# Three score banks allocated once and rotated by hand, with one head's exp and the other head's scores issued in two parts

## The chip, the cores and the metric

The kernel runs on one core of a Trainium2 chip. The metric is the device time of one execution in microseconds (us), and a version's time is the median of several runs. The engines are named as in the profile: PE (TensorE matmuls), PEld (its weight loads), DVE (VectorE), ACT (ScalarE), POOL (GpSimd) and SP (SyncE, which issues DMAs).

## The reference

Eight sequences of 1024 tokens with 256 features go through a causal attention of 16 heads of 16 features, and then through a mixture of 8 experts of which each token takes 2. All is float32. Cut to what matters:

```python
x = x + layernorm(attention(layernorm(x)))
    # q, k, v = x Wq^T, x Wk^T, x Wv^T, split into 16 heads of 16
    # score = q k^T / 4, causal; attn = softmax(score); out = (attn v) Wo^T
x = x + layernorm(moe(layernorm(x)))
    # scores = softmax(x Wr^T + br); the 2 best of 8 experts
    # gate, up = x Wgu[e] + bgu[e]; gate = min(gate, 7); up = clip(up, -7, 7)
    # down = ((up + 1) * gate * sigmoid(1.702 gate)) Wd[e] + bd[e], weighted by the scores
```

## The kernel before

The work has two parts. Attention comes first (to about 1395 us of the profile), with the routing of the tokens woven into it; then the experts' tiles follow.

In attention the unit of work `u` is one sequence and a group of four heads: 8 sequences by 4 groups are 32 units. The four heads of a group lie on four groups of 32 rows of PE, so that four matmuls with 32 rows each can run side by side. Each unit is gone through twice, one unit apart. The first pass (`maxima_tiles`, tiles `sa`, matmul L834) makes scores with queries on partitions, and DVE takes the row maxima (L844, L850, L859, L865); with them goes an edge copy on ACT (L869). The maxima become one more row of the queries `qP` by a DMA (L807). The second pass (`values_tiles`, tiles `sb`, matmul L929) makes the scores again, with keys on partitions and the maximum already subtracted; ACT takes the exp (L941) out of the score bank into the tile `pT` in the on-chip memory, POOL masks the diagonal blocks (L950), and PE multiplies by the values (L970, `weighted`), one or more steps later.

A unit has nine steps (`STEPS`): two EDGE steps, three TWO steps and four WHOLE steps. In an EDGE or a WHOLE step, each head has one score matmul of 512 columns in the second pass; in a TWO step it has two, of 384 and 128 or of 256 and 256 columns, that share one bank. Each step is done for two pairs of heads. One pass through the inner loop (L1328 to L1341) therefore issues a set of four heads: two of `sa` of unit `u` and the other two of `sb` of unit `u - 1`, in the order sa head 0, sa head 1, sb head 0, sb head 1. Then ACT's exps of the set are issued, and after them the reductions and the edge copy of `sa`. Between sets PE gets `av` matmuls and pieces of side jobs (projections L740, values L726, output projection L1031, transposes L574 and L1092, routing).

The order of PE, DVE, ACT and SP is the order of the source: the attention part is a list written out by the loop, in which side jobs are put in by estimated costs and due times (`pump`, `spend`). These estimates are not measured in the run, so the order is fixed when the kernel is built. POOL's order is held to the source by added dependencies (`in_order`).

The scores of `sb` and all the side jobs' PSUM tiles come from one pool, `ps_b` (L540), of three buffers of one PSUM bank (512 float32 for each of 128 partitions):

```python
ps_b = ctx.enter_context(tc.tile_pool(name="ps_b", bufs=3, space=PSUM))
...
banks = [
    ps_b.tile([P, QC], F32, tag="b", name=f"sb_{u}_{k}_{2 * pair + hh}")
    for hh in range(2)
]
...
for hh in range(2):
    nc.scalar.activation(pT[:, 2 * pair + hh, :], banks[hh], AF.Exp)
```

The pool hands out its three buffers in turn. A set takes two of them; so where no side job takes one in between, the second `sb` head of a set gets the bank that the first `sb` head of the set before had, and waits until its exp has read it. Where one side job took a bank in between, the two heads get the banks of the same heads of the set before. In the last unit the second pair of heads uses a bank pair of another pool (`ps_a`) and one exp of 1024 columns (L938). The experts' part goes on using `ps_b` for its second product (`dn`, L1497).

Of the kernel before, what the change touches and what calls it, by code (L numbers as in the profile page):

```python
# [11 lines left out]
F32 = mybir.dt.float32  # L12
# [5 lines left out]
P = 128  # L18
# [40 lines left out]
def attn_moe_kernel(  # L59
# [241 lines left out]
    def table(nr):  # L301
# [56 lines left out]
        yield piece(pe=0.6, dve=0.2, after=3 if first_ones else 5)  # L358
        ps = ps_b.tile([P, 3], F32, tag="b", name=f"segps_{nr}")
        if first_ones:  # L360
# [8 lines left out]
        yield piece(pe=0.3, dve=0.9, after=2)  # L369
        ps = ps_b.tile([P, 3], F32, tag="b", name=f"firstps_{nr}")  # L370
        nc.tensor.matmul(ps[:, 0:2], lhsT=before, rhs=seg[:, 0:2], start=True, stop=True)
# [43 lines left out]
        yield piece(pe=0.5, dve=0.6, after=2 if first_ones else 5)  # L415
        ps = ps_b.tile([P, 2, NTILES], F32, tag="b", name=f"tabps_{nr}")
        nc.tensor.matmul(
# [8 lines left out]
        if first_ones:  # L426

            yield piece(dve=0.9)
            some = tp.tile([P, 1], F32, tag="some", name=f"some_{nr}")
            nc.vector.tensor_scalar(  # L430
                some, ends[:, 0:1], -1.0, float(EARLY), ALU.mult, ALU.add
            )
            nc.vector.tensor_scalar(some, some, 0.0, seg[:, 0:1], ALU.max, ALU.min)
            each = tp.tile([P, E], F32, tag="each", name=f"each_{nr}")
            nc.vector.tensor_scalar(each, of_e, some, None, ALU.mult)
            yield piece(pe=0.3, dve=0.2, after=1)
            ps = ps_b.tile([P, E], F32, tag="b", name=f"takenps_{nr}")
            nc.tensor.matmul(ps, lhsT=ones, rhs=each, start=True, stop=True)
            nc.vector.tensor_copy(taken, ps)
# [99 lines left out]

    ps_b = ctx.enter_context(tc.tile_pool(name="ps_b", bufs=3, space=PSUM))  # L540

    with ExitStack() as attn:
# [28 lines left out]
        def turn_x(b, t, xn, kt):  # L571
            ps = ps_b.tile([P, NTB, P], F32, tag="b", name=f"xps_{b}_{t}_{kt}")
            for n in range(NTB):
                nc.tensor.transpose(ps[:, n, :], xn[:, n, ts(kt, P)], ident)  # L574
            nc.scalar.copy(xnTs[b][:, kt, ts(t, TB)], ps.rearrange("p n c -> p (n c)"))

        def weights(name, wr, kt):

            ps = ps_b.tile([P, KT, P], F32, tag="b", name=f"wps_{name}_{kt}")
            for ot in range(KT):  # L580
                nc.tensor.transpose(ps[:, ot, :], wr[:, ot, ts(kt, P)], ident)
            nc.scalar.activation(
                wT[name][:, kt, :], ps.rearrange("p t o -> p (t o)"), AF.Copy,
                scale=DH**-0.5 if name == "q" else 1.0,
            )
# [82 lines left out]
        def others(wr):  # L668
# [14 lines left out]
            yield piece(pe=0.3, dve=0.2)  # L683
            ps = ps_b.tile([P, KT, E], F32, tag="b", name="rps")
            for kt in range(KT):
                nc.tensor.transpose(ps[:, kt, :], rwr[:, ts(kt, P)], ident[:E, :E])
            nc.vector.tensor_copy(rw32[:, :, :E], ps)
            yield piece(pe=0.2, dve=0.4)
            ps = ps_b.tile([P, E * 2 * FT], F32, tag="b", name="gubps")
            nc.tensor.transpose(ps, gubr, ident[: E * 2 * FT, : E * 2 * FT])  # L690
# [27 lines left out]
        def values(b):  # L718

            xnT = xnTs[b]  # L720
            for n2 in range(NB // 2):
                yield piece(pe=1.75, act=0.6, after=0 if n2 else 1)
                ps = ps_b.tile([P, 2, D], F32, tag="b", name=f"vps_{b}_{n2}")
                for k in range(2):
                    for kt in range(KT):
                        nc.tensor.matmul(  # L726
                            ps[:, k, :], lhsT=xnT[:, kt, ts(2 * n2 + k, P)], rhs=wT["v"][:, kt, :],
                            start=(kt == 0), stop=(kt == KT - 1),
                        )
                nc.scalar.copy(  # L730
                    vps[b % 2][:, ts(n2, 2), : H * VS].rearrange(
                        "p n (h c) -> p n h c", c=VS
                    )[:, :, :, :DH],
                    ps.rearrange("p n (h d) -> p n h d", d=DH),
                )

        def project_chunk(b, g2, name, c):
            ps = ps_b.tile([P, QC], F32, tag="b", name=f"pj{name}_{b}_{g2}_{c}")
            for kt in range(KT):
# [159 lines left out]
        def values_tiles(u):  # L899
# [11 lines left out]
            def pair_of_heads(k, pair):  # L911
# [3 lines left out]
                if u == B * NG - 1 and pair:  # L915
                    both = ps_a.tile([P, 2, QC], F32, tag="a", name=f"sb_{u}_{k}_{pair}")
                    banks = [both[:, hh, :] for hh in range(2)]
                else:
                    banks = [
                        ps_b.tile([P, QC], F32, tag="b", name=f"sb_{u}_{k}_{2 * pair + hh}")  # L920
                        for hh in range(2)
                    ]

                def scores(hh, part):
                    if part == len(STEPS[k][2]):
                        return
                    c, j, off, at = list(parts(k))[part]
                    r = ds((2 * pair + hh) * HS, HS)
                    nc.tensor.matmul(  # L929
                        banks[hh][:, ds(at, QC - off)], lhsT=kP[r, ts(j, P)],  # L930
                        rhs=qP[r, ds(c * QC + off, QC - off)],
                        start=True, stop=True,
                    )

                def exps():
                    if u == B * NG - 1 and pair:

                        nc.scalar.activation(pT[:, ts(pair, 2), :], both, AF.Exp)  # L938
                        return
                    for hh in range(2):  # L940
                        nc.scalar.activation(pT[:, 2 * pair + hh, :], banks[hh], AF.Exp)  # L941

# [74 lines left out]
        def finish(b, c):  # L1017
# [8 lines left out]
            for n2 in range(NTB // 2):  # L1026
                yield piece(pe=1.75, act=0.6, after=0 if n2 else 2)
                ps = ps_b.tile([P, 2, D], F32, tag="b", name=f"yps_{b}_{c}_{n2}")
                for k in range(2):
# [44 lines left out]
        def route(t, x1, last):  # L1074
# [13 lines left out]
            for kt in range(KT):  # L1088
                yield piece(pe=0.5, act=0.6, after=0 if kt else 2)
                ps = ps_b.tile([P, NTB, P], F32, tag="b", name=f"x2ps_{t}_{kt}")  # L1090
                for n in range(NTB):
# [3 lines left out]
            yield piece(pe=0.6, act=0.3, after=1 + 2 * more)  # L1095
            ps = ps_b.tile([P, P], F32, tag="b", name=f"lpsT_{t}")
            for kt in range(KT):
# [7 lines left out]
            yield piece(pe=0.2, dve=0.2, after=1 + more)  # L1105
            lps = ps_b.tile([P, NTB, HS], F32, tag="b", name=f"lps_{t}")
            nc.tensor.transpose(lps.rearrange("p n r -> p (n r)"), lgT, ident)
# [42 lines left out]
            yield piece(pe=0.6, dve=0.2, after=1 + 4 * more)  # L1150
            cps = ps_b.tile([P, 2, NTB, E], F32, tag="b", name=f"cps_{t}")
            for k, m in enumerate((before, ones)):
# [335 lines left out]
    def lower_half(i, act, wd, bs, final=False):  # L1488
# [7 lines left out]
        else:  # L1496
            ps = ps_b.tile([P, TN, D], F32, tag="b", name=f"dn_{i}")  # L1497
            pss = [ps[:, n : n + 1, :] for n in range(TN)]
# [263 lines left out]
```

## Time and profile before

| what | value |
|---|---|
| median of 3 runs | 2196.28 us (2194.48 to 2196.68) |
| the profiled execution | 2198.81 us, span 2197.1 us |
| mean granted PE clock | 0.978 |
| instructions in the span | 44652 |
| exps of 512 columns (L941) | 1134, mean 596 ns, 616.6 us busy |
| matmul records of `sb` (L929) | 3072, 717.1 us busy |
| matmul records of `sa` (L834) | 3072, 658.7 us busy |
| ACT waiting for L929 before L941 | 361.2 us |
| PE's first waiting weight load of L929 for L941 | 20.3 us in 32 waits |

The span is the time from the first to the last instruction of the profiled execution; its own time is 1.7 us longer. A float32 matmul leaves two records, one for each pass over its columns. An instruction's length includes its way through the engine, so two that follow each other on one engine overlap in the records. A wait is listed only where the engine stood idle; PE is busy as long as any of its row groups works.

### The profile page before, as it was taken

Reading aid. Unit: us, or ns where it says so; the run is one execution under the profiler, and the core shown is the slowest. Engines: PE = TensorE matmul, PEld = TensorE weight load, DVE = VectorE, ACT = ScalarE, POOL = GpSimd, SP = SyncE. Lnnn points to the kernel's source line nnn. Section 1 sums busy time; section 2 is a strip of 40 time slices with the busy share of each in tenths; the row PEclk is TensorE's granted clock in tenths of the full one; section 3 lists DMA queues with packets and bytes.
Section 4 is the critical chain, followed back from the end, with each engine's and each line's share of the span. In section 5 each row is a group of like instructions: output and inputs, shape, how many; then the busy total and the mean of one; then the engine's idle time right before and its main releaser. Section 6 shows DMA issues by size and latency. Waiting matters only on the chain.

```text
span 2197.1 us, 44652 instructions
## 1 busy us (share of the span) xinstructions
PE 2085.6 (95%) x16205; PEld 1273.3 (58%) x16205; DVE 1713.9 (78%) x4090; ACT 1061.2 (48%) x2068; POOL 1058.0 (48%) x1217
## 2 busy tenths in 40 slices
PE   7999999999999999999999988899999999999995
PEld 4444444444444444444434433577788888888884
DVE  4786887887896886886887788567868888877776
ACT  3566665666666655665655654423123232222222
POOL 3421742572564455465454445455545444444443
PEclk9999999999999999999999998999999999999998
DMA  4101112111212112111112111645777767776784
GB/s 122 22 17 42 39 26 57 36 50 36 48 43 50 29 37 64 27 48 46 48 36 55 29 47 35 201 167 201 227 262 255 280 241 271 277 247 223 271 273 157
DMA packets 147096, 254.85 MB, mean 116 GB/s; under 512 B 21504, under 2 KB 106008, under 8 KB 144952
## 3 DMA queue, kind: packets, MB, share of 16 engines
q1 hardware_dynamic: 133128, 217.01, 32.1%
q0 software_dynamic: 12528, 34.36, 4.2%
q8 instruction: 129, 2.11, 0.4%
q14 instruction: 95, 0.78, 0.1%
q10 hardware_dynamic: 1216, 0.58, 0.1%
HBM read 171.13 MB, written 55.63 MB: 103 GB/s over the span
## 4 chain that ended last, share of the span: by engine, by line
PE 67%; DVE 20%; POOL 6%; issue 4%; ACT 1%; DMA 1%; another core or an unknown queue 0%; SPq 0%; DVEq 0%; ACTq 0%; POOLq 0%
PE sa L834 18%; PE gu L1461 13%; PE av L970 10%; PE dn L1501 7%; PE sb L929 6%; PE pjk L740 3%; PE yps L1031 3%; PE vps L726 3%; PE pjq L740 3%; DVE mx L850 2%; DVE sa L844 2%; DVE acc L1576 1%; POOL ytd L1514 1%; DVE gate L1470 1%; DVE act L1482 1%
## 5 line engine op out<-in xcount | busy, mean ns | idle before, releaser
L941 ACT ACTIVATE pT<-sb 128x512 f32<-128x512 f32 x1134 | 616.6, 596 | 399.8 <-PE sb L929 361.2
L929 PE MATMUL sb<-qP,kP 32*128 32x512 f32 (+3 forms) x3072 | 717.1, 530 | 11.3 <-ACT pT L941 6.5
L834 PE MATMUL sa<-kP,qP 32*128 32x512 f32 (+3 forms) x3072 | 658.7, 529 | 23.5 <-DVE mx L844 10.8
L1461 PE MATMUL gu<-xsT,wg 128*128 128x256 f32 (+1 forms) x2208 | 488.9, 374 | 5.8 <-DVE act L1482 3.7
L1461 PEld LDWEIGHTS gu<-xsT,wg 128*128 128x128 f32 x2208 | 409.3, 191 | 61.6 <-ACT sig L1472 4.1
L850 DVE TENSOR_REDUCE mx<-sa 128x2 f32<-128x1024 f32 x256 | 310.9, 1216 | 127.0 <-PE sb L929 100.6
L950 POOL TENSOR_SCALAR_AFFINE_SELECT pT<-pT 128x512 f32<-128x512 f32 x256 | 163.1, 652 | 474.7 <-ACT pT L941 462.1
L834 PEld LDWEIGHTS sa<-kP,qP 32*128 32x128 f32 x3072 | 228.8, 186 | 247.5 <-issue 104.7
L1472 ACT ACTIVATE sig<-gate 128x256 f32<-128x256 f32 (+1 forms) x276 | 112.8, 409 | 531.6 <-DVE gate L1470 485.6
L970 PE MATMUL av<-pT,vpad 128*32 128x256 f32 (+1 forms) x5120 | 350.1, 370 | 5.9 <-DVE avs L981 4.3
L929 PEld LDWEIGHTS sb<-qP,kP 32*128 32x128 f32 x3072 | 298.6, 187 | 54.8 <-ACT pT L941 20.3
L1477 POOL TENSOR_TENSOR sig<-sig,gate 128x256 f32<-128x256 f32 (+1 forms) x276 | 198.7, 722 | 256.3 <-ACT sig L1472 253.9
L970 PEld LDWEIGHTS av<-pT,vpad 128*32 128x32 f32 x5120 | 116.8, 109 | 296.5 <-issue 238.7
L1501 PE MATMUL dn<-wd,act 128*128 128x256 f32 x1064 | 263.0, 387 | 13.8 <-DVE act L1482 13.3
L1470 DVE TENSOR_SCALAR gate<-gu,bs 128x256 f32<-128x256 f32 (+1 forms) x276 | 128.9, 467 | 124.7 <-PE gu L1461 110.0
L1501 PEld LDWEIGHTS dn<-wd,act 128*128 128x128 f32 x1064 | 197.1, 193 | 48.1 <-DVE act L1482 24.2
L844 DVE CUSTOM_DVE_ANT_0 sa<-sa,cmask 128x512 f32<-128x512 f32 x256 | 177.7, 698 | 43.0 <-PE sb L929 20.8
L1514 POOL DMA_INDIRECT ytd<-ys,places x133 | 133.8, 1006 | 130.1 <-DVE ys L1509 93.8
L1194 POOL DMA_INDIRECT xsd<-xn,slots x128 | 127.9, 999 | 64.0 <-DVE xn L1190 34.0
L1482 DVE SCALAR_TENSOR_TENSOR act<-up,sig 128x256 f32<-128x256 f32 (+1 forms) x276 | 123.2, 446 | 27.1 <-POOL sig L1477 27.1
L869 ACT COPY edge<-sa 128x512 f32<-128x512 f32 x192 | 113.0, 589 | 35.8 <-DVE mx L859 16.5
L517 POOL TENSOR_TENSOR rstd<-ve,nhalf_seg 128x4 f32<-128x4 f32 x48 | 50.2, 1045 | 163.3 <-DVE ve L512 161.6
(243 smaller groups left out, 2416.8 us busy)
## 6 DMA issues: line engine op xcount, KB each, us to landing
wg<-_L_ffn_gate_up_proj_dram SPq DMA_DIRECT2D x69, 1024.0 KB
wd<-in_L_ffn_down_proj_dram SPq DMA_DIRECT2D x69, 512.0 KB
xs<-xsd SPq DMA_DIRECT2D x60, 258.0 KB
yy<-ytd SPq DMA_DIRECT2D x15, 1024.0 KB
bs<-biasd SPq DMA_DIRECT2D x69, 132.0 KB
x<-in_L_attn_x_dram SPq DMA_DIRECT2D x16, 512.0 KB
aT<-avn SPq DMA_DIRECT2D x256, 32.0 KB
x1d<-y SPq DMA_DIRECT2D x16, 512.0 KB
```

Of the source, the lines that this page charges most:

```text
L834: nc.tensor.matmul(ps[:, hh, ds(at, w)], lhsT=qP[r, ts(i, P)], rhs=kP[r, ds(c * QC, w)], start=True, stop=True,)
L844: nc.vector.tensor_tensor_reduce(out=ps[:, hh, :], in0=ps[:, hh, :], in1=cmask, scale=1.0, scalar=NEG, op0=ALU.add, op1=ALU.max, accum_out ...
L850: nc.vector.tensor_reduce(mx[:, heads, i, 2:3], ps, AX.X, ALU.max)
L929: nc.tensor.matmul(banks[hh][:, ds(at, QC - off)], lhsT=kP[r, ts(j, P)], rhs=qP[r, ds(c * QC + off, QC - off)], start=True, stop=True,)
L941: nc.scalar.activation(pT[:, 2 * pair + hh, :], banks[hh], AF.Exp)
L950: in_order(nc.gpsimd.affine_select(out=d, in_=d, compare_op=ALU.is_ge, fill=0.0, base=0, pattern=[[0, HG], [1, P]], channel_multiplier=-1,))
L970: nc.tensor.matmul(av[ds(hh * HS, HS), ds(off + a - at, z - a)], lhsT=vp[:, j, ds((g * HG + hh) * VS, HS)], rhs=pT[:, hh, a:z],  start=c n ...
L1461: nc.tensor.matmul(ps[:, half, :w], lhsT=wg[:, kt, ds(half * FF + f * P, P)], rhs=xT[:, kt, :], start=(kt == 0), stop=(kt == KT - 1),)
L1470: nc.vector.tensor_scalar(gt, ps[:, 0, :w], bs[:, f : f + 1], LIMIT, ALU.add, ALU.min)
L1477: in_order(nc.gpsimd.tensor_tensor(sg, sg, gt, ALU.mult))
L1501: nc.tensor.matmul(pss[n][:, 0, :], lhsT=act[:, f, ts(n, P)], rhs=wd[:, f, :], start=(f == 0), stop=(f == FT - 1),)
L1514: put = nc.gpsimd.indirect_dma_start(out=yt_dram[:, :], out_offset=bass.IndirectOffsetOnAxis(ap=places[:, i, n : n + 1], axis=0), in_=y[:, ...
```

## The change

The pool `ps_b` gets one buffer, and three tiles of a whole bank are taken from it once, at the start. A function `bank` hands out the first of them, cut to the shape asked for, and moves it to the end of the row. Every place that took a tile from `ps_b` calls it instead (side jobs, routing, `sb` and `dn`).

In `values_tiles` the exp of the first head of a pair is issued as two instructions of 256 columns each, in all steps. The scores of the second head of a pair are issued as two matmuls of 256 columns each where the step has one part (EDGE and WHOLE); in a TWO step they stay as they were. The exp of the second head stays one instruction of 512 columns.

```diff
-    ps_b = ctx.enter_context(tc.tile_pool(name="ps_b", bufs=3, space=PSUM))
+    ps_b = ctx.enter_context(tc.tile_pool(name="ps_b", bufs=1, space=PSUM))
+    banks = deque(ps_b.tile([P, 2 * D], F32, name=f"bank{i}") for i in range(3))
+
+    def bank(parts, *free):
+        at = banks[0]
+        banks.rotate(-1)
+        size = 1
+        for n in free:
+            size *= n
+        at = at[:parts, :size]
+        if len(free) == 2:
+            return at.rearrange("p (a b) -> p a b", b=free[1])
+        if len(free) == 3:
+            return at.rearrange("p (a b c) -> p a b c", b=free[1], c=free[2])
+        return at
...
-            ps = ps_b.tile([P, QC], F32, tag="b", name=f"pj{name}_{b}_{g2}_{c}")
+            ps = bank(P, QC)
...
-                    banks = [
-                        ps_b.tile([P, QC], F32, tag="b", name=f"sb_{u}_{k}_{2 * pair + hh}")
-                        for hh in range(2)
-                    ]
+                    into = [bank(P, QC) for hh in range(2)]
+                half = QC // 2
+
+                def pieces(hh, part):
+                    c, j, off, at = list(parts(k))[part]
+                    if hh and len(STEPS[k][2]) == 1:
+                        return [(c, j, off, at, half), (c, j, off + half, at + half, half)]
+                    return [(c, j, off, at, QC - off)]
 
                 def scores(hh, part):
                     if part == len(STEPS[k][2]):
                         return
-                    c, j, off, at = list(parts(k))[part]
                     r = ds((2 * pair + hh) * HS, HS)
-                    nc.tensor.matmul(
-                        banks[hh][:, ds(at, QC - off)], lhsT=kP[r, ts(j, P)],
-                        rhs=qP[r, ds(c * QC + off, QC - off)],
-                        start=True, stop=True,
-                    )
+                    for c, j, off, at, w in pieces(hh, part):
+                        nc.tensor.matmul(
+                            into[hh][:, ds(at, w)], lhsT=kP[r, ts(j, P)],
+                            rhs=qP[r, ds(c * QC + off, w)],
+                            start=True, stop=True,
+                        )
...
-                    for hh in range(2):
-                        nc.scalar.activation(pT[:, 2 * pair + hh, :], banks[hh], AF.Exp)
+                    for at in range(2):
+                        nc.scalar.activation(
+                            pT[:, 2 * pair, ts(at, half)], into[0][:, ts(at, half)], AF.Exp
+                        )
+                    nc.scalar.activation(pT[:, 2 * pair + 1, :], into[1], AF.Exp)
```

More of the change, by code (lines that the diff above doesn't have):

```diff
@@ L358, in table @@
         yield piece(pe=0.6, dve=0.2, after=3 if first_ones else 5)
-        ps = ps_b.tile([P, 3], F32, tag="b", name=f"segps_{nr}")
+        ps = bank(P, 3)
         if first_ones:
@@ L369, in table @@
         yield piece(pe=0.3, dve=0.9, after=2)
-        ps = ps_b.tile([P, 3], F32, tag="b", name=f"firstps_{nr}")
+        ps = bank(P, 3)
         nc.tensor.matmul(ps[:, 0:2], lhsT=before, rhs=seg[:, 0:2], start=True, stop=True)
@@ L415, in table @@
         yield piece(pe=0.5, dve=0.6, after=2 if first_ones else 5)
-        ps = ps_b.tile([P, 2, NTILES], F32, tag="b", name=f"tabps_{nr}")
+        ps = bank(P, 2, NTILES)
         nc.tensor.matmul(
@@ L436, in table @@
             yield piece(pe=0.3, dve=0.2, after=1)
-            ps = ps_b.tile([P, E], F32, tag="b", name=f"takenps_{nr}")
+            ps = bank(P, E)
             nc.tensor.matmul(ps, lhsT=ones, rhs=each, start=True, stop=True)
@@ L571, in turn_x @@
         def turn_x(b, t, xn, kt):
-            ps = ps_b.tile([P, NTB, P], F32, tag="b", name=f"xps_{b}_{t}_{kt}")
+            ps = bank(P, NTB, P)
             for n in range(NTB):
@@ L577, in weights @@
         def weights(name, wr, kt):
-            ps = ps_b.tile([P, KT, P], F32, tag="b", name=f"wps_{name}_{kt}")
+            ps = bank(P, KT, P)
             for ot in range(KT):
@@ L683, in others @@
             yield piece(pe=0.3, dve=0.2)
-            ps = ps_b.tile([P, KT, E], F32, tag="b", name="rps")
+            ps = bank(P, KT, E)
             for kt in range(KT):
@@ L688, in others @@
             yield piece(pe=0.2, dve=0.4)
-            ps = ps_b.tile([P, E * 2 * FT], F32, tag="b", name="gubps")
+            ps = bank(P, E * 2 * FT)
             nc.tensor.transpose(ps, gubr, ident[: E * 2 * FT, : E * 2 * FT])
@@ L722, in values @@
                 yield piece(pe=1.75, act=0.6, after=0 if n2 else 1)
-                ps = ps_b.tile([P, 2, D], F32, tag="b", name=f"vps_{b}_{n2}")
+                ps = bank(P, 2, D)
                 for k in range(2):
@@ L916, in pair_of_heads @@
                     both = ps_a.tile([P, 2, QC], F32, tag="a", name=f"sb_{u}_{k}_{pair}")
-                    banks = [both[:, hh, :] for hh in range(2)]
+                    into = [both[:, hh, :] for hh in range(2)]
                 else:
-                    banks = [
-                        ps_b.tile([P, QC], F32, tag="b", name=f"sb_{u}_{k}_{2 * pair + hh}")
-                        for hh in range(2)
-                    ]
+                    into = [bank(P, QC) for hh in range(2)]
[5 more added lines that the diff above has]
+                    return [(c, j, off, at, QC - off)]
                 def scores(hh, part):
@@ L1027, in finish @@
                 yield piece(pe=1.75, act=0.6, after=0 if n2 else 2)
-                ps = ps_b.tile([P, 2, D], F32, tag="b", name=f"yps_{b}_{c}_{n2}")
+                ps = bank(P, 2, D)
                 for k in range(2):
@@ L1089, in route @@
                 yield piece(pe=0.5, act=0.6, after=0 if kt else 2)
-                ps = ps_b.tile([P, NTB, P], F32, tag="b", name=f"x2ps_{t}_{kt}")
+                ps = bank(P, NTB, P)
                 for n in range(NTB):
@@ L1095, in route @@
             yield piece(pe=0.6, act=0.3, after=1 + 2 * more)
-            ps = ps_b.tile([P, P], F32, tag="b", name=f"lpsT_{t}")
+            ps = bank(P, P)
             for kt in range(KT):
@@ L1105, in route @@
             yield piece(pe=0.2, dve=0.2, after=1 + more)
-            lps = ps_b.tile([P, NTB, HS], F32, tag="b", name=f"lps_{t}")
+            lps = bank(P, NTB, HS)
             nc.tensor.transpose(lps.rearrange("p n r -> p (n r)"), lgT, ident)
@@ L1150, in route @@
             yield piece(pe=0.6, dve=0.2, after=1 + 4 * more)
-            cps = ps_b.tile([P, 2, NTB, E], F32, tag="b", name=f"cps_{t}")
+            cps = bank(P, 2, NTB, E)
             for k, m in enumerate((before, ones)):
@@ L1496, in lower_half @@
         else:
-            ps = ps_b.tile([P, TN, D], F32, tag="b", name=f"dn_{i}")
+            ps = bank(P, TN, D)
             pss = [ps[:, n : n + 1, :] for n in range(TN)]
```

## The prediction

> **What bounds the kernel now.** I read the busy shares first, then the stage that the change touches, then the chain of waits in it, and last the order of events inside one step. Busy shares and stages come from the page and the busy time by stretches (columns: stretch, its length, then busy time and instructions of PE, PEld, DVE, ACT, POOL, then granted clock, DMA share, GB/s):
>
> ```profile
> PE 2085.6 (95%) x16205; PEld 1273.3 (58%) x16205; DVE 1713.9 (78%) x4090; ACT 1061.2 (48%) x2068; POOL 1058.0 (48%) x1217
> ...
> 60.00:400.00 340.00, 332.06 (x3254) 157.43 (x3250) 270.59 (x560) 218.00 (x407) 137.39 (x156) 0.99 0.16 35
> 400.00:800.00 400.00, 390.70 (x3740) 181.12 (x3736) 331.62 (x749) 249.87 (x467) 206.71 (x225) 1.00 0.17 41
> ```
>
> Scores with exps (L929, L941) run from 60 to about 1395 us. In the two stretches shown PE is busy 98% of the time and ACT 62 to 64%. So PE is the bound, and ACT has room on average. The chain of waits over 60 to 1395 us says the same:
>
> ```profile
> by line: PE sa L834 28.4%; PE av L970 16.4%; PE sb L929 9.8%; PE vps L726 4.2%; PE yps L1031 4.2%; PE pjk L740 4.0%; PE pjq L740 4.0%; DVE mx L850 3.7%; DVE sa L844 2.9%; issue 2.7%; POOL pT L950 1.6%; DVE mx L888 1.4%; PE xps L574 1.2%; PO
> ```
>
> The PE lines shown sum to 72%. ACT does not appear, and that misleads, because a wait can hide inside a busy PE. One PE step is a set of four heads' scores that run side by side on four row groups: two heads of sa, two of sb. Two sets in order of time (start, length, engine, line; then ACT):
>
> ```profile
> 627.58 0.70 PE L834 MATMUL sa<-kP,qP 32*128 32x512 f32 x2
> 627.60 0.70 PE L929 MATMUL sb<-qP,kP 32*128 32x512 f32 x2
> ...
> 628.65 0.64 PE L970 MATMUL av<-pT,vpad 128*32 128x256 f32 x8
> 629.22 0.70 PE L834 MATMUL sa<-kP,qP 32*128 32x512 f32 x2
> 629.24 0.93 PE L929 MATMUL sb<-qP,kP 32*128 32x512 f32 x2
> ...
> 630.53 0.64 PE L970 MATMUL av<-pT,vpad 128*32 128x256 f32 x8
> ...
> 628.83 1.08 ACT L941 ACTIVATE pT<-sb 128x512 f32<-128x512 f32 x2 [0.99 <-PE sb L929]
> ```
>
> The first set takes 628.65 - 627.58 = 1.07 us. The second takes 630.53 - 629.22 = 1.31: its sb row is 0.93 long, not 0.70, because the second head started 0.23 late. Its bank was held by the previous pair's first exp, which began at 628.83 and takes 0.597. PE counts as busy all the while, so the list of waits (idle time alone) misses most of this. I therefore counted single records: for each set, the second head's first weight load against the end of the exp that its semaphore names. Without the last group of heads there are 558 sets. In **237** the load follows that exp's end within 60 ns: the set is held. 188 are held by a first head's exp, 49 by a second head's. The lateness sums to 67.9 us. In 43 more the exp had ended only 60 to 140 ns before.
>
> **The change part by part.** The order of the built kernel differs from before in two counts alone: ACT has 567 exps more, PE 384 matmuls more. With those folded together, all five engines issue the same sequence; nothing moves past anything on SP, POOL or DVE, and no DMA changes.
>
> *The banks by hand.* Rotation is the same three banks in the same turn. I compared which instruction each semaphore wait names, before and after. The waits between engines that carry the loop are the same. What goes are waits of PE on its own old writes (46 on sb) and some long-met ones; what comes are likewise waits on instructions several steps back. Separate waiting instructions on PE go from 516 to 509; one takes 51 ns in the trace, so 0.4 us. I cost this at nothing; the cover is that such waits were met long ago.
>
> *The point of the two parts.* It would be that the second head's first half enters a bank when half of it is read. In the built kernel that does not happen: every one of the 566 matmul waits that name a first-head exp names its **second** part; only one weighted-values matmul at the very end waits for a first part. The first half of the scores waits for both parts, the second half has no wait of its own. So the stall's cause stays and its exp is longer.
>
> The skill has a rule against the idea itself. The Trainium skill, "PSUM — Partial Sum Buffer", section "PSUM bank collisions raise a hardware error", says to guard PSUM by bank and quadrant, not by address, because TensorE writing a bank while ScalarE reads other columns of it is an error. No run here shows a collision. By that rule nothing is gained by the early start and the sum stays the one below; guarded by address it would be that of the last rival.
>
> *The exp in two parts.* No 128x256 exp from a score bank is in the trace. Nearest rows are two 128x256 ACTIVATEs in a row from PSUM (L582), and two 128x512 exps in a row (1.08 above, 0.597 each, so the second starts 0.493 after the first):
>
> ```profile
> 24.63 0.67 ACT L582 ACTIVATE wvT<-wps_v 128x256 f32<-128x256 f32 x2
> 25.27 0.67 ACT L582 ACTIVATE woT<-wps_o 128x256 f32<-128x256 f32 x2
> ...
> L582 ACT ACTIVATE woT<-wps_o 128x256 f32<-128x256 f32 x2 | 0.7, 383 | 0.0
> ```
>
> Two take 0.67 at 0.383 each, so the second starts 0.286 after the first. The first head's exp ends after 0.67, not 0.597: **0.073 later**. The second head's exp starts 2 x 0.286 = 0.572 after, not 0.493: 0.079 later. Lower end: no fixed part at all, 0. Upper end: parts that do not overlap, 2 x 0.384 - 0.597 = 0.171. I take 0.073 and 0.079, since the L582 row has this form.
>
> *The scores in two parts.* 384 sets have one row group with four 256-column passes for two 512-column ones. A set made wholly of 256-column passes is in the trace:
>
> ```profile
> 509.88 0.48 PE L834 MATMUL sa<-kP,qP 32*128 32x256 f32 x2
> ...
> 510.96 0.70 PE L740 MATMUL pjq<-xnT,wqT 128*128 128x512 f32 x1
> ```
>
> It takes 1.08; over all such sets the shortest is 1.075, against 1.070 for 512. So 0.005 each. Lower end 0; upper end 0.064 (their median, 1.134, which holds waits of other kinds).
>
> *Behind the longer exps on ACT* stand the copies of edges (L869) and of projections. The list of waits has the next sa waiting 29 times for an edge copy; those come 0.079 later. Other copies have the idle time of ACT as cover.
>
> Sum: 188 x 0.073 = 13.7; 49 x 0.079 = 3.9; the 43 close ones become held where under 125 ns were left, 0.9 in all; 384 x 0.005 = 1.9; 29 x 0.079 = 2.3. Together 22.7. Off this: 101 of the held sets follow a held set at once. There the earlier lateness delays the start of the next set but not the exp it waits for, so up to 101 x 0.075 = 7.6 is not paid again; I take half, 3.8. Of 18.9 about three quarters stand on the path, as PE does in the chain: **14 us**. On the profiled execution's own 2198.8 (span 2197.1 and 1.7 around it) that gives 2212.8; the runs' median, 2196.28, is 2.5 lower, so I predict **2210**.
>
> **The rivals.**
>
> *Absorbed* (0 to 6 us, 2196 to 2202). All 101 relieved, the rest met by DVE, which is 80 to 83% busy there and also holds sets. For: DVE and POOL lines in the chain. Against: 136 held sets follow one that was not held.
>
> *Dearer* (20 to 40 us, 2217 to 2236). Parts of one bank do not overlap: 237 x 0.171 = 40.5, plus 1.9. Or ACT's added 567 x 0.079 = 45 us falls in stretches where ACT is behind, and each held set pays twice. For: in 49 sets the second head's exp decides. Against: the L582 row, and ACT would go only from about 62% to 65%.
>
> *Faster: the halves do overlap* (2183). In 137 one-part sets held by a first head's exp, the second head would start when the first part ends, 0.384 for 0.597, 0.213 earlier: 29 us, within the 51 us of lateness of one-part sets, while the remaining terms, 22.7 - 137 x 0.073 = 12.7, stay. Net 16.5, three quarters of it 12 to 13. It decides from the point where a matmul's semaphore names the first part. None does, so this is nearly excluded; some chance is left for an effect I do not see.
>
> **How the numbers follow.** Forecast (2203 to 2217) 0.62, absorbed 0.18, dearer 0.15, faster 0.05. Range 2199 to 2230: all of the forecast, half of absorbed and two thirds of dearer. It leaves out the end where parts never overlap (2239). About 0.2% (4.4 us) is what a measurement can tell from no change: of absorbed 0.14 lies within it and 0.04 above. So slower 0.62 + 0.15 + 0.04 = 0.81, same 0.14, faster 0.05.
>
> **What would show it.** Right: no gap between the two parts of the first exp other than some 0.29 between their starts; held sets still begin some 50 ns after the *second* part ends; unheld sets take 1.07 to 1.08; PE's matmul records in L929's place grow by 768; MoE part (from 1395) as long as before. Wrong: second heads that start after the first part; held sets much fewer; a time under 2196, or over 2230, where I would look for parts that run one after the other, or for sets that became longer without an exp holding them.

## The result, and the profile after

| what | before | after |
|---|---|---|
| median of 5 runs | 2196.28 us (2194.48 to 2197.45) | 2205.36 us (2203.94 to 2211.63) |
| profiled execution, span | 2198.81, 2197.1 us | 2205.36, 2203.6 us |
| mean granted PE clock | 0.978 | 0.980 |
| first to last of the 558 sets | | 11.7 us longer |
| after the last set (experts) | 834.7 us | 831.7 us |

The change makes the kernel slower: ratio **1.0052 [1.0039, 1.0065]**, 9.1 us between the medians. The experts' part took 3.0 us less in the profiled execution; the records of the granted clock show 43.7 us of it at half clock before and 37.7 after, and a set that lies wholly in half clock takes 2.02 us in before where a free one takes 1.07. By that ratio 6.0 us less of it is worth about 3 us, an estimate. The first set also began 2.3 us earlier; 11.7 - 2.3 - 3.0 is the 6.5 us by which the span grew, to rounding. So the change acts in the attention part alone.

First the busy shares of the page of after (engine, busy time, share of the span, instructions):

```profile
PE 2087.5 (95%) x16973; PEld 1414.2 (64%) x16973; DVE 1712.5 (78%) x4090; ACT 1094.8 (50%) x2635; POOL 1058.2 (48%) x1217
```

PE has 768 records more (two passes for each of 384 matmuls) and 1.9 us more busy time; ACT has 567 instructions and 33.6 us more. Now the stretches of the attention part in after (length, then busy time and instructions of PE, PEld, DVE, ACT, POOL, then clock, DMA share, GB/s):

```profile
60.00:400.00 340.00, 331.63 (x3412) 191.87 (x3413) 267.25 (x552) 223.99 (x552) 134.03 (x153) 0.98 0.16 35
400.00:800.00 400.00, 391.75 (x3949) 225.50 (x3946) 328.68 (x740) 257.75 (x633) 205.45 (x224) 1.00 0.17 42
```

PE is still at 98% and ACT only at 64 to 66%. By shares nothing has happened. The chain of waits over 60 to 1402 us of after doesn't name ACT either, but the scores of the second pass (`sb`, both heads; now L948) rise from 9.8% to 16.6% of it:

```profile
by line: PE sa L849 23.0%; PE av L992 16.7%; PE bank L948 16.6%; PE bank L755 8.1%; PE bank L1053 4.2%; PE bank L741 3.8%; DVE mx L865 3.3%; issue 2.9%; DVE sa L859 2.4%; POOL pT L972 1.7%; DVE mx L903 1.3%; POOL edge L898 1.2%; PE bank L58
```

One set that runs free and one that is held, in after, by order of events (start, length, engine, line):

```profile
633.39 0.70 PE L849 MATMUL sa<-kP,qP 32*128 32x512 f32 x2
633.41 0.70 PE L948 MATMUL bank<-qP,kP 32*128 32x512 f32 x3
...
634.47 0.64 PE L992 MATMUL av<-pT,vpad 128*32 128x256 f32 x8
635.04 0.70 PE L849 MATMUL sa<-kP,qP 32*128 32x512 f32 x2
635.05 0.77 PE L948 MATMUL bank<-qP,kP 32*128 32x512 f32 x2
...
635.59 0.89 PE L948 MATMUL bank<-qP,kP 32*128 32x512 f32 x4
636.40 0.64 PE L992 MATMUL av<-pT,vpad 128*32 128x256 f32 x8
```

and ACT beside it, the exps of the pair before:

```profile
634.64 0.66 ACT L960 ACTIVATE pT<-bank 128x256 f32<-128x256 f32 x2 [0.93 <-PE bank L948]
635.18 0.60 ACT L963 ACTIVATE pT<-bank 128x512 f32<-128x512 f32 x1
```

The free set takes 634.47 - 633.39 = 1.08 us. The held one takes 636.40 - 635.04 = 1.36, where its like took 1.31 before. The two parts of the exp end at 634.64 + 0.66 = 635.30, and by the single records the second head's first weight load starts at 635.348, 48 ns later. The first part has been done since 635.02, by the 0.382 of the row below; this didn't let PE start. The groups of after (columns: busy, mean ns of one, then the idle time before and what ended it):

```profile
L948 PE MATMUL bank<-qP,kP 32*128 32x512 f32 (+1 forms) x3780 | 728.1, 455 | 20.2 <-ACT pT L960 13.3
...
L960 ACT ACTIVATE pT<-bank 128x256 f32<-128x256 f32 x1134 | 374.0, 382 | 387.1 <-PE bank L948 336.9
...
L963 ACT ACTIVATE pT<-bank 128x512 f32<-128x512 f32 x567 | 343.8, 606 | 9.1 <-PE bank L948 7.5
```

Each first exp now costs two instructions of 382 ns, whose starts are 0.280 us apart. By single records the pair lasts 0.658 us where one exp lasted 0.597, and the second head's exp starts 0.543 after the first part, not 0.493 after the first exp.

Counted over the same 558 sets as in the prediction, 236 are held (187 by a first head's exp, 49 by a second head's) where 237 were; the summed lateness of the second heads goes from 67.9 to 81.4 us. Some 4 of these 13.5 us lie in the eight or nine held sets that half clock touches; in the others the lateness goes from 61.5 to 70.8. So the stalls are the same in number and each is a little longer.

### The profile page after: what moved, and what is told of

It is laid out like the page before. It is cut to its first block, busy times and chain, and to the rows that moved or that the text cites. A ratio compares the mean times of both kernels' runs of the same rounds, so it can differ in the third digit from the quotient of the medians.

```text
span 2203.6 us, 46769 instructions
## 1 busy us (share of the span) xinstructions
PE 2087.5 (95%) x16973; PEld 1414.2 (64%) x16973; DVE 1712.5 (78%) x4090; ACT 1094.8 (50%) x2635; POOL 1058.2 (48%) x1217
## 4 chain that ended last, share of the span: by engine, by line
PE 69%; DVE 17%; POOL 6%; issue 4%; ACT 2%; DMA 1%; another core or an unknown queue 0%; SPq 0%; DVEq 0%; ACTq 0%; POOLq 0%
PE sa L849 15%; PE gu L1483 13%; PE av L992 10%; PE bank L948 10%; PE bank L1523 7%; PE bank L755 6%; PE bank L1053 3%; PE bank L741 3%; DVE mx L865 2%; DVE sa L859 2%; DVE acc L1598 1%; POOL ytd L1536 1%; DVE gate L1492 1%; POOL xsd L1216 1%; DVE act L1504 1%
## 5 line engine op out<-in xcount | busy, mean ns | idle before, releaser
L948 PE MATMUL bank<-qP,kP 32*128 32x512 f32 (+1 forms) x3780 | 728.1, 455 | 20.2 <-ACT pT L960 13.3
L849 PE MATMUL sa<-kP,qP 32*128 32x512 f32 (+3 forms) x3072 | 658.1, 528 | 21.1 <-DVE mx L859 11.8
L960 ACT ACTIVATE pT<-bank 128x256 f32<-128x256 f32 x1134 | 374.0, 382 | 387.1 <-PE bank L948 336.9
L948 PEld LDWEIGHTS bank<-qP,kP 32*128 32x128 f32 x3780 | 444.8, 187 | 91.1 <-ACT pT L960 28.9
L963 ACT ACTIVATE pT<-bank 128x512 f32<-128x512 f32 x567 | 343.8, 606 | 9.1 <-PE bank L948 7.5
L1523 PE MATMUL bank<-wd,act 128*128 128x256 f32 x1056 | 258.9, 385 | 12.7 <-DVE act L1504 11.9
L1523 PEld LDWEIGHTS bank<-wd,act 128*128 128x128 f32 x1056 | 195.1, 192 | 45.4 <-DVE act L1504 21.8
L903 DVE TENSOR_REDUCE mx<-edge 128x8 f32<-128x1024 f32 x96 | 115.9, 1208 | 17.7 <-POOL edge L898 17.1
```

Source lines behind the costliest of these rows:

```text
L849: nc.tensor.matmul(ps[:, hh, ds(at, w)], lhsT=qP[r, ts(i, P)], rhs=kP[r, ds(c * QC, w)], start=True, stop=True,)
L948: nc.tensor.matmul(into[hh][:, ds(at, w)], lhsT=kP[r, ts(j, P)], rhs=qP[r, ds(c * QC + off, w)], start=True, stop=True,)
L960: nc.scalar.activation(pT[:, 2 * pair, ts(at, half)], into[0][:, ts(at, half)], AF.Exp)
L963: nc.scalar.activation(pT[:, 2 * pair + 1, :], into[1], AF.Exp)
L1523: nc.tensor.matmul(pss[n][:, 0, :], lhsT=act[:, f, ts(n, P)], rhs=wd[:, f, :], start=(f == 0), stop=(f == FT - 1),)
```

## The experiments

The theory to test, **held**: the second head of a set waits for the whole first exp, so the time follows how much later that exp ends. Its rivals: **ACT work** (567 more instructions delay the copies that PE waits for), **PE passes** (more and shorter matmuls), and **the banks** (the hand-made order makes other waits).

Two measures are used besides the ratio, both from the traces' single records. The *lateness* is the sum counted above. The *full-clock difference* comes from the time between the first weight loads of a set and the next one, kernel against kernel, summed over the intervals that lie clear of any record of half clock, by some 2 us on either side, in both executions. Counted without that margin the differences below move by up to 1.3 us. The measure is needed because the granted clock isn't the same from chip to chip. The kernel before takes 2196 us on the chip of the result and 2149 to 2150 us where most experiments ran. The stretch from 800 to 1200 us of before shows a part of the reason, first on the chip of the result, then on the other:

```profile
800.00:1200.00 400.00, 383.99 (x3550) 179.64 (x3552) 317.77 (x743) 233.71 (x437) 201.82 (x219) 0.97 0.17 45
```

```profile
800.00:1200.00 400.00, 392.24 (x3804) 186.34 (x3801) 337.08 (x769) 253.34 (x474) 224.62 (x241) 1.00 0.19 47
```

The columns are those of the stretches above; the clock is 0.97 on the one and 1.00 on the other. From the first set to the last before takes 45.2 us more on the chip of the result, and some 19 of these lie in intervals at full clock, in about 25 large steps. Their cause stays open. Every ratio below is against the kernel before on the same chip.

| kernel | ratio [95%] | medians, this and before | held | lateness | full-clock difference |
|---|---|---|---|---|---|
| before_again | 1.0000 [0.9989, 1.0012] | 2150.05, 2149.37 | 231 | 46.4 | 0 |
| after_again | 1.0033 [1.0021, 1.0045] | 2156.64, 2149.37 | 238 | 56.5 | +7.1 |
| banks_by_hand | 1.0018 [1.0005, 1.0030] | 2153.54, 2149.95 | 231 | 45.2 | -0.2 |
| banks_again | 1.0009 [0.9996, 1.0021] | 2150.84, 2149.37 | 232 | 45.3 | +0.3 |
| exp_two | 1.0051 [1.0035, 1.0067] | 2161.70, 2149.95 | 235 | 55.7 | +6.4 |
| scores_two | 1.0002 [0.9990, 1.0015] | 2150.06, 2149.95 | 234 | 45.4 | +0.3 |
| exp_second_two | 1.0023 [1.0011, 1.0035] | 2155.53, 2149.95 | 229 | 46.7 | +4.4 |
| second_again | 1.0018 [1.0003, 1.0032] | 2199.35, 2195.42 | 226 | 64.6 | see there |
| exp_four | 1.0111 [1.0096, 1.0126] | 2174.49, 2149.13 | 262 | 81.0 | +24.0 |
| exp_turned | 1.0082 [1.0069, 1.0095] | 2167.51, 2149.37 | 299 | 62.9 | +17.1 |
| turned_by_hand | 1.0630 [1.0616, 1.0644] | 2283.37, 2149.13 | 359 | 204.5 | +135.5 |
| exp_short | 0.9968 [0.9957, 0.9980] | 2142.01, 2149.13 | 193 | 25.0 | -11.3 |

The differences (us) are against the trace of before_again. The runs with 2149.95 us for before ran on another chip than before_again, with nearly the same time. second_again ran where before takes 2195.42 us, like the chip of the result; before's own lateness there is the 67.9 above.

### The three parts of the change, each alone

**banks_by_hand** is the changed kernel with the exps and the scores whole again (the scores' part of the diff is left out here):

```diff
...
-                    for at in range(2):
-                        nc.scalar.activation(
-                            pT[:, 2 * pair, ts(at, half)], into[0][:, ts(at, half)], AF.Exp
-                        )
-                    nc.scalar.activation(pT[:, 2 * pair + 1, :], into[1], AF.Exp)
+                    for hh in range(2):
+                        nc.scalar.activation(pT[:, 2 * pair + hh, :], into[hh], AF.Exp)
```

> Only the three banks kept by hand; exps and scores whole as before. The theory that held banks are the cost (a longer first exp keeps the bank that the second head's scores wait for), the rival that ACT's added work is the cost, and the rival that PE's added passes are the cost all say no change: 2196 us, within 3 us. The rival that the hand-kept banks bring other waits says slower by 3 to 9 us.

Measured: 3.6 us more between the medians, but -0.2 at full clock: what it lost lies at half clock (+2.6). It was repeated, see banks_again.

**exp_two** is the kernel before, pool and all, with the first head's exp in two parts:

```diff
-                    for hh in range(2):
-                        nc.scalar.activation(pT[:, 2 * pair + hh, :], banks[hh], AF.Exp)
+                    half = QC // 2
+                    for at in range(2):
+                        nc.scalar.activation(
+                            pT[:, 2 * pair, ts(at, half)], banks[0][:, ts(at, half)], AF.Exp
+                        )
+                    nc.scalar.activation(pT[:, 2 * pair + 1, :], banks[1], AF.Exp)
```

> The pool as before, scores whole, only the first head's exp in two parts. Held banks: nearly all of the change's cost, 6 to 8 us slower (2202 to 2204), and the exp of the first head ends about 0.065 us later. ACT's added work: the same 6 to 8 us. PE's passes or hand-kept banks as the cost: no change.

Measured: 1.0051, as much as the whole change (1.0052, and 1.0033 for after_again). That is 11.8 us between the medians and 6.4 at full clock, where 6 to 8 were expected. The loss is spread: some 165 intervals differ by 0.02 to 0.08 us, nearly all of them later, and these sum to nearly 8 us. Its exps, in the groups of exp_two by shape, last as long as in after:

```profile
L942 ACT ACTIVATE pT<-sb 128x256 f32<-128x256 f32 x1134 | 373.8, 382 | 349.1 <-PE sb L929 340.1 <-PE sa L834 2.9 <-POOL pT L954 2.3
```

The exp of the first head in two parts carries the cost, without the banks by hand and without the second head's parts.

exp_two brings one thing that the change doesn't: 976 separate waiting instructions on PE in the built kernel, where before has 516 and the changed kernel 509. The added ones wait for PE's own old writes. They cost nothing that the trace shows. In the intervals at full clock, 295 have such a wait added and no held head; their median is unchanged and they sum to -0.8 us. Another 181 have both; these are later by 0.060 us at the median, 7.1 us in all.

**scores_two** is the kernel before with the second head's scores in two parts (EDGE and WHOLE steps):

```diff
+                    cut = 2 if hh and len(STEPS[k][2]) == 1 else 1
+                    w = (QC - off) // cut
+                    for n in range(cut):
...
-                            banks[hh][:, ds(at, QC - off)], lhsT=kP[r, ts(j, P)],
-                            rhs=qP[r, ds(c * QC + off, QC - off)],
+                            banks[hh][:, ds(at + n * w, w)], lhsT=kP[r, ts(j, P)],
+                            rhs=qP[r, ds(c * QC + off + n * w, w)],
```

> The pool as before, exps whole, only the second head's scores in two matmuls. Held banks: 384 sets by 0.005 us, three quarters on the path, 1 to 2 us slower (2197 to 2199). PE's added passes and weight loads as the cost: 5 to 9 us slower. ACT's added work as the cost: no change.

Measured: nothing at 0.2%. In the groups of scores_two by shape the 256-column passes stand beside the rest:

```profile
L932 PE MATMUL sb<-qP,kP 32*128 32x256 f32 x2048 | 506.9, 404 | 0.0
```

Of these, 1536 are new (384 x 4). The shortest set is 1.075 us long (1.070 before), and the intervals that differ by up to 0.02 us sum to +1.1 us: PE passes cost about 1 us.

**exp_second_two** is exp_two with the second head's exp in two parts in place of the first's: the same 567 instructions more on ACT, but the first head's bank comes free as early as before.

```diff
-                    for hh in range(2):
-                        nc.scalar.activation(pT[:, 2 * pair + hh, :], banks[hh], AF.Exp)
+                    half = QC // 2
+                    nc.scalar.activation(pT[:, 2 * pair, :], banks[0], AF.Exp)
+                    for at in range(2):
+                        nc.scalar.activation(
+                            pT[:, 2 * pair + 1, ts(at, half)], banks[1][:, ts(at, half)], AF.Exp
+                        )
```

> The pool as before, scores whole, the second head's exp in two parts and the first head's whole: the same number of added ACT instructions as with the first head's. Held banks: only the 49 sets that a second head's exp holds get later, by 0.065 us, and what stands behind on ACT: 2 to 3 us slower (2198 to 2199). ACT's added work: as much as with the first head's exp in two, 6 to 8 us slower.

Measured: 5.6 us between the medians and +4.4 us at full clock, less than exp_two and more than held allowed. The lateness is 46.7, as before, and all steps under 0.4 us sum to -0.4 us here, where exp_two has 7.1. So this is another loss, of eight larger steps that sum to 5.0 us. The list of waits has the next sa waiting 40 times for an edge copy, 23.6 us in all, where before_again has 31 times and 17.9 us. exp_two and after_again have no more of that wait than before (17.5 in 31, 18.0 in 32). What the large steps are is looked into below, with second_again.

### The change once more, beside a control

**before_again** is the kernel before as it is, **after_again** the changed kernel as it is, **banks_again** the same as banks_by_hand.

> The kernel before, measured against itself, for the scatter of the comparison and for a profile on the same chip as the runs beside it. Every theory: ratio 1, within 0.15%.

> The whole change on the same chip as the control beside it. Held banks: 0.35 to 0.55% slower, of which the sets outside stretches of half clock carry at least two thirds. The rival that most of the cost is more throttling of the PE clock: as much slower, but with the sets at full clock no more than 3 us later in all.

> Only the banks by hand once more; it came out 0.18% slower than the kernel before, with no later sets at full clock. Held banks, and the view that the difference was the PE clock's throttling by chance: ratio within 0.15% of 1 this time. The rival that hand-kept banks cost something of their own: again 0.1 to 0.3% slower, with the loss at the same places.

Measured: the control is at 1.0000, after_again at 1.0033 and banks_again at 1.0009, its interval with 1 in it. In after_again 161 intervals differ by 0.02 to 0.08 us, nearly all of them later, 7.8 us in all (155 and 7.4 on the chip of the result), and the whole way from the first set to the last is 7.7 us longer. The banks by hand show no cost at full clock in either run (-0.2, +0.3); what they lost the first time lay in stretches at half clock, and was not there the second time.

### The hold made longer

**exp_four** is exp_two with four parts of 128 columns:

```diff
-                    for hh in range(2):
-                        nc.scalar.activation(pT[:, 2 * pair + hh, :], banks[hh], AF.Exp)
+                    for at in range(4):
+                        nc.scalar.activation(
+                            pT[:, 2 * pair, ts(at, P)], banks[0][:, ts(at, P)], AF.Exp
+                        )
+                    nc.scalar.activation(pT[:, 2 * pair + 1, :], banks[1], AF.Exp)
```

> The pool as before, scores whole, the first head's exp in four parts of 128 columns. From 597 ns for 512 columns and 383 for 256, four parts end about 0.17 us later than one, 2.6 times as late as two parts did. Held banks: 2.6 times the 7 to 11 us of two parts, 18 to 28 us slower (0.85 to 1.3%). If only the sets just at the edge paid: no more than 12 us.

Measured: 1.0111, 24.0 us at full clock. A first exp in exp_four, then a held set:

```profile
637.72 0.79 ACT L941 ACTIVATE pT<-sb 128x128 f32<-128x128 f32 x4 [0.80 <-PE sb L929]
638.36 0.63 ACT L944 ACTIVATE pT<-sb 128x512 f32<-128x512 f32 x1
```

```profile
638.12 0.70 PE L834 MATMUL sa<-kP,qP 32*128 32x512 f32 x2
638.13 1.12 PE L929 MATMUL sb<-qP,kP 32*128 32x512 f32 x2
...
639.61 0.64 PE L973 MATMUL av<-pT,vpad 128*32 128x256 f32 x8
```

The four parts end 0.79 after the start, 0.188 later than one exp; the set takes 639.61 - 638.12 = 1.49. The end moved 0.188/0.061 = 3.1 times as far as in exp_two, and the intervals that changed by less than 0.4 us sum to 23.1 us, 3.3 times exp_two's 7.1. By this count the cost grows about as the delay of the exp's end does; with the larger steps it is 24.0 to 6.4, or 3.8 times.

### The order of the two exps turned

**exp_turned** takes the second head's exp first, with the pool of before:

```diff
-                    for hh in range(2):
+                    for hh in (1, 0):
                         nc.scalar.activation(pT[:, 2 * pair + hh, :], banks[hh], AF.Exp)
```

> The pool as before, scores and exps whole, but ACT takes the second head's exp ahead of the first head's: the same instructions on every engine, and the first head's bank comes free some 0.49 us later. Held banks: 187 sets by up to 0.49 us and some 180 close ones by half of that, about 0.6 of it on the path: 40 to 90 us slower. ACT's added work or PE's added passes as the cost: no change, since nothing is added.

Measured: 18.1 us, not 40 to 90. The expectation took the pool to hand out its banks in a fixed turn, as the section on the kernel before says. It doesn't: in the built kernel 558 score matmuls wait for the *second* head's exp, where 558 waited for the first head's. The pool hands out what was released first, so the turned order turned the banks with it, and no bank came free later. (In the kernel before the two rules nearly agree: of 1461 steps from one taken bank to the next, 1449 keep the fixed turn.) 299 sets are held instead of 231, with 16.5 us more lateness beside 17.1 us at full clock. That now the late head of one set holds the next, so that a delay is handed on, is argued and not tested by itself.

**turned_by_hand** is the same turn in banks_by_hand, where the rotation is fixed:

```diff
-                    for hh in range(2):
+                    for hh in (1, 0):
                         nc.scalar.activation(pT[:, 2 * pair + hh, :], into[hh], AF.Exp)
```

> The second head's exp ahead of the first head's, now with the three banks by hand, so that the next set's second head really gets the bank that comes free 0.49 us later (with the pool the turn of the buffers had followed the order of release). The same instructions on every engine. Held banks: 50 to 110 us slower (2.3 to 5%). ACT's added work or PE's added passes as the cost: no change, since nothing is added.

Measured: **1.0630**, 134 us and more than expected, with the same work on every engine as before. ACT and a held set in turned_by_hand:

```profile
644.84 1.08 ACT L953 ACTIVATE pT<-bank 128x512 f32<-128x512 f32 x2 [0.67 <-PE bank L941]
```

```profile
645.21 0.70 PE L849 MATMUL sa<-kP,qP 32*128 32x512 f32 x2
645.22 0.69 PE L941 MATMUL bank<-qP,kP 32*128 32x512 f32 x1
...
645.75 1.34 PE L941 MATMUL bank<-qP,kP 32*128 32x512 f32 x3
647.03 0.64 PE L982 MATMUL av<-pT,vpad 128*32 128x256 f32 x8
```

The bank is now free only when both exps are done (644.84 + 1.08 = 645.92), and the set takes 647.03 - 645.21 = 1.82 us, though PE shows no gap. All 359 holds are by the first head's exp, half of them longer than 0.655 us. Neither ACT's work nor PE's passes changed, and exp_turned has the same order on ACT for 18.1 us, so this is the bank's release alone.

### The hold made shorter

**exp_short** asks what an early release would bring at most: in one-part steps the first head's exp reads only its first 256 columns.

```diff
+                    short = len(STEPS[k][2]) == 1
                     for hh in range(2):
-                        nc.scalar.activation(pT[:, 2 * pair + hh, :], banks[hh], AF.Exp)
+                        w = QC // 2 if short and not hh else QC
+                        nc.scalar.activation(pT[:, 2 * pair + hh, :w], banks[hh][:, :w], AF.Exp)
...
```

> Leaves work out: in one-part steps the first head's exp takes only the first 256 columns, and the weighted values read these twice; everything else as before. It prices what a first part that frees the bank by itself could have brought. Held banks: the first head's exp ends 0.21 us earlier in two thirds of the sets, 10 to 25 us faster (0.5 to 1.2%). Were held banks not what the change touches, but only ACT's load: ACT is not the bound, within 3 us of no change.

Measured: 0.9968, 7.1 us between the medians, 11.3 at full clock; expected were 10 to 25. In the groups of exp_short by shape:

```profile
L943 ACT ACTIVATE pT<-sb 128x256 f32<-128x256 f32 x378 | 145.4, 385 | 289.5 <-PE sb L929 288.5
```

These 378 exps end 0.21 us earlier. The held sets fall from 231 to 193 and the lateness by 21.4 us, and only about half of that reaches the time. What holds the rest of these sets instead was not measured.

### The other ACT split once more

**second_again** is exp_second_two as it was.

> The second head's exp in two parts once more. The first time it came out 5 us slower, while the sets at full clock were no later in all and the trace lost its time before the first sets and in stretches of half clock. Held banks: 0 to 3 us slower (ratio 1.000 to 1.0014), the sets at full clock within 1 us of the control's. ACT's added work: 6 to 8 us slower, as with the first head's exp in two.

Measured, on the slower chip: 3.9 us, between what held and ACT work asked for. Against the trace of before on the chip of the result it is +1.7 us at full clock and +3.6 elsewhere. That division is loose: without the margin around half clock it is +9.6 and -4.3. The expectation says of the first run that the sets at full clock were no later in all; counted as in the table they are 4.4 us later.

The wait of sa for edge copies is again longer: 20.5 us in 38 waits, 15.4 in 29 before. The largest steps are in the same places in both runs (units 18 and 22, EDGE step 3 and the TWO step after it, +0.58 to +0.64 each; in exp_second_two also unit 26). There DVE comes late, beside POOL. In exp_second_two, DVE, then POOL, ahead of the steps of unit 22:

```profile
969.77 0.58 DVE L1179 TENSOR_TENSOR pick<-is_r,slot 128x64 f32<-128x64 f32 x1
...
970.64 1.02 DVE L1185 CAST slots<-sf 128x8 int32<-128x8 f32 x1
```

```profile
969.04 1.23 POOL L954 TENSOR_SCALAR_AFFINE_SELECT pT<-pT 128x512 f32<-128x512 f32 x2 [1.16 <-ACT pT L943]
970.53 1.10 POOL L883 TENSOR_SCALAR_AFFINE_SELECT edge<-edge 128x1024 f32<-128x1024 f32 x1 [0.26 <-ACT edge L869]
```

and the same in before_again:

```profile
964.85 0.20 DVE L1175 TENSOR_TENSOR pick<-is_r,slot 128x64 f32<-128x64 f32 x1
...
965.34 0.25 DVE L1181 CAST slots<-sf 128x8 int32<-128x8 f32 x1
```

```profile
964.34 1.23 POOL L950 TENSOR_SCALAR_AFFINE_SELECT pT<-pT 128x512 f32<-128x512 f32 x2 [1.37 <-ACT pT L941]
965.61 1.10 POOL L883 TENSOR_SCALAR_AFFINE_SELECT edge<-edge 128x1024 f32<-128x1024 f32 x1
```

`pick` and the conversion `slots` (a CAST) belong to the routing. In the built kernel of exp_second_two 104 of POOL's diagonal masks of `pT` wait for the second head's *first* part, where the same 104 wait for its whole exp in before. So the masks begin earlier: counted from the first load of the second set of step 2 they start at 2.17 us instead of 2.60. `pick` now starts early in the second mask, not at the end of the first, and takes 0.58 us instead of 0.20. That puts the conversion at 3.77 instead of 3.61, behind the start of POOL's edge mask (3.66 instead of 3.88). Where POOL starts before the conversion, this lasts 1.02 us and ends with POOL's; where it starts after, 0.25. The edge copy is no later here; it starts at 3.01 instead of 3.23.

The six steps sum to 3.6 of exp_second_two's 4.4 us at full clock. So most of what the split second exp loses isn't ACT's work making copies late, but masks that start early beside DVE. This is read from the order of events; no run holds the masks back by themselves, and why the list has more waits for edge copies stays open. It isn't what the change lost: in after and in exp_two the 104 masks wait for the whole second exp, as in before.

## Why the prediction was right, point by point

**The hidden wait bounds the gain and the loss: right.** The lateness moves with the time in both directions: -21.4 us of lateness goes with -11.3 us at full clock, +9.3 with +6.4, +10.1 with +7.1, +16.5 with +17.1, +34.6 with +24.0, +158.1 with +135.5. Only the split of the second exp falls out of line (+0.3 with +4.4, and -3.3 with +1.7 in second_again), with steps of its own where DVE is late beside POOL.

**The banks by hand cost nothing: right** at full clock in two runs, and within 0.2% by the medians, the first time hardly so.

**The halves don't help: right.** Held sets start some 50 ns after the second part's end, and their number stayed (237 and 236). The rule of the Trainium skill that the prediction weighed ("PSUM — Partial Sum Buffer", section "PSUM bank collisions raise a hardware error") agrees with that: the built kernel guards the whole bank. What a release by parts of one bank would do was not tried, since PE would write a bank that ACT reads.

**The size of the exp's delay: mis-sized.** The prediction had 0.073 for the end and 0.079 for the second head's start; 0.061 and 0.050 were measured. The first comes from the L582 pair, whose starts were 0.286 apart (0.280 here). The second went wrong by doubling that: an exp of 512 columns starts 0.543 - 0.280 = 0.263 after the part ahead of it, less than a part after a part.

**The other terms.** PE: 384 x 0.005 = 1.9 was forecast, some 1 us measured. Edge copies: 29 x 0.079 = 2.3 was forecast, and none of it is there (15.4 us of that wait before, 13.8 after; 17.9 and 18.0 on the other chip). With the second exp split that wait is longer, but the large steps there are DVE's, not the copies'. Close sets: 0.9 was forecast for those that become held, but the number of held sets hardly grew (237 and 236 here; 231 to 238 and 235 in after_again and exp_two).

**The sum.** With the measured sizes the prediction's own terms give 188 x 0.061 + 49 x 0.050 = 13.9, with PE's 1.0 and less the 3.8 of relief 11.1, and three quarters of that 8.3 us. 9.1 and 7.3 us were measured on the two chips. The relief and the share of three quarters stood for what held sets pass on; on the second chip the sets grew by 10.9 us in all (662.7 to 673.6) and the way from first to last by 7.7, a share of 0.71. The forecast of 14 us was too high mainly by the exps' and the edges' terms.

**The rivals.** *Absorbed* ends at 6 us, and the result on the chip of the prediction is above it; that 237 held sets made only some 160 intervals longer is the part of it that is true. *Dearer* fell: the parts overlap by 0.1 us. *Faster* fell by its mechanism, and exp_short shows that it was overpriced as well: 29 us gross was the forecast for releasing one-part sets early, 7 to 11 us came from doing the equivalent with less work for ACT.

**What stays open:** why exp_turned's holds are more in number, what makes before slower at full clock on the chip of the result, and how much of the intervals that changed by over 0.4 us there is the clock's: these sum to 3.0 us without the margin and to 0.1 with it.

## What to carry to other kernels

A wait can sit inside a busy engine: where several instructions run side by side, take each one's start against the event that it waits for, since the list of waits shows idle time alone (20.3 us of 67.9 here). Splitting an instruction that empties a bank, when the bank is released as a whole, only delays the release here; the price was the later end of the last part, times the sets that were held, times a share below one for what they pass on. Before building on an early release, look up in the built kernel which instruction the waiting one names, and measure the gain's upper end by leaving the work out.

## What the runs showed of the hardware

Of the exp's time a part doesn't shrink with the columns: one of 512, 256 and 128 columns lasts 597, 382 and 284 ns, and in a row the starts of the last two are 0.280 to 0.281 and 0.157 to 0.174 us apart.

A DVE conversion of 8 columns to int32 takes 0.17 us at the median and up to 1.02 when it starts behind the start of a POOL mask of 1024 columns; it then ends 0.03 after the mask. The Trainium skill, "Advanced Engine Details and Errata", section "VectorE Performance Modes", has a note that DVE's second port to the on-chip memory is shared with GpSimd, so that they block each other; it gives no size, and the runs show up to 0.85 us for one instruction.

Between the first and the last set the granted clock falls to half for 3.4, 6.8 or 10.2 us at a time, and by chip: the kernel before has 47.8 us of it there on the chip of the result and 20.5 on the other. A change of a few us that is spread over many sets can be read from the intervals at full clock where the medians scatter by as much; large steps next to half clock can't be told from it.
